# A two-layer graph network on one core: second pass in a written order, a third column block by lists, comparisons moved to ScalarE

## The chip, the cores and the metric

The kernel runs on one core of one Trainium2 chip. The metric is the device time of one execution in microseconds, the median over several executions. A profile is one further execution, recorded by the hardware profiler; its time is given beside the others.

The engines are named as the profile names them: PE is TensorE (matrix products; PEld its weight loads), DVE is VectorE, ACT is ScalarE, POOL is GpSimd, SP is SyncE. SP, ACT and POOL also issue DMA transfers, each from its own queue, in the order of the program; every engine executes its own instructions in the order in which they were issued to it.

## The reference

Two layers over a graph of 3327 nodes with 512 features each. The adjacency matrix is sparse, with weights, and skewed: the first nodes are hubs. It has ones of self-loops on its diagonal before it is weighted.

```python
def reference(x, adj, W1, b1, W2, b2, W_sa, a_sa, W_gcnb, b_gcnb, Wa, ba, Wb, bb):
    # layer 0
    h = relu(layernorm(x))
    x = x + adj @ (relu(adj @ (h @ W1) + b1) @ W2) + b2
    # layer 1
    h = relu(layernorm(x))
    t = adj @ h
    attn_a = sigmoid(concat([t, h], 1) @ Wa.T + ba)
    attn_b = sigmoid(concat([t, h], 1) @ Wb.T + bb)
    hw = h @ W_sa
    s = (hw @ a_sa[0, :512])[:, None] + (hw @ a_sa[0, 512:])[None, :]
    e = where(adj != 0, exp(-leaky_relu(s, 0.01)), 0)
    x_a = e / (e.sum(1, keepdims=True) + 1e-5) @ hw
    x_b = adj @ (h @ W_gcnb) + b_gcnb
    return x + sigmoid(attn_a * x_a + attn_b * x_b)
```

`W1` is 512 x 128, so the hidden width of layer 0 is 128.

## The kernel before

The nodes are padded to 3328, which is 26 blocks of 128. The adjacency comes transposed (`adjT`, rows are sources). Its columns, the target nodes, are cut into chunks of 512 from the back: six of 512 and one of 256 (blocks 0 and 1). Everything is float32, and PE runs a float32 matmul as two records in the profile.

**First pass** (`back` loop, lines 540 to 600). Per chunk, 26 matmuls `acc_u` (line 568) add `u = relu(layernorm(x)) @ W1` over all sources. In the first chunk the rows of `u` are made on the way (lines 322 to 336). Each adjacency tile of 128 x 512 is loaded once by SP (line 271). DVE takes from every tile the largest absolute value of each group of 32 targets (`most`, line 572). From this, `make_lists` makes for each group the list of sources that have an edge into it: flags, a running sum, a comparison of places with offsets (`at`, line 502, on DVE), small bf16 matmuls (`p_list`, line 513), then row numbers `row_h` and `row_a`. It is a generator; one step runs after each matmul of the next chunk. At a chunk's end ACT makes the Relu and `make_g` stores the block's `g` rows.

**Lists and gathers.** With the lists, POOL gathers by indirect DMA (line 166): `ae` gets the adjacency values of the listed sources (16 KB a gather), `g_row` the rows of `g` (64 KB), and in layer 1 `hr` or `rows` the rows of the finished layer (260 KB). `rooms` says how many places of 64 sources each block's list has per half: 8 for block 1, down to 3 for the last. The blocks of `OWN` load the sources of their own block directly and leave them out of the list (`extra`). If a list were longer than its places, a flag would start a dense fallback at the end (`over`, from line 1141).

**Second pass** (lines 801 to 860). It computes `adj @ g` for the seven chunks. `LISTED = 2` chunks of the back are summed by lists (`list_sums`, `acc_s`, line 784), the other five densely (`acc_g`, line 825, 26 matmuls each). Between the matmuls of a chunk, generators work on the chunk before: `make_h1` multiplies by `W2` (`px`, line 663), adds x and the bias (lines 650, 666), stores the row, makes layernorm and Relu through `ln_relu` (lines 232 to 245: statistics on DVE, root on ACT), then four weighted sums on DVE: right and left attention score (line 623) and the two gate logits of the node itself (line 630). `add_hubs` adds each finished row into the sums of block 0, which has edges from nearly everywhere (`acc_hub`, line 709, two matmuls a row, 26 rows), and `make_e_hub` makes the attention weights for it. Which generator advances is settled by remainders of the counter n, for instance `n % 3 == 2`; the scheduler may still move PE instructions against one another where nothing orders them. x is loaded when its row's turn is near (up to three rows ahead in a chunk).

**Attention stage** (from line 865). For block 25 down to block 1: `attend` gathers the rows, makes the weights on DVE and ACT; `sums` adds rows (`acc`, line 981); `copy_out` and `turn` transpose the sums (`ptt`, line 995, copied by DVE at line 1010); `weigh` multiplies by the output weights (`p_b`, line 1035, and `p_a`, line 1042); `finish` makes gates, tanh and the output. These steps are software-pipelined over blocks by hand (`queued` makes an instruction issue behind another on its engine). Remaining adjacency gathers are fetched two a block (`AE_PER`), and row gathers run 3 or 4 blocks ahead (`LEAD`).

Of the kernel before, what the change touches and what calls it, by code (L numbers as in the profile page):

```python
# [18 lines left out]
P = 128  # L19
# [6 lines left out]
EH = 8  # L26
SEG = 4
WAKE = 14
LISTED = 2
LN_EPS = 1e-5  # L30
SUM_EPS = 1e-5
SLOPE = 0.01

# [5 lines left out]
LATE = 10, 11, 16  # L39

OWN = 1, 6, 7, 8, 12, 13, 14, 15, 17, 18


def list_rooms(n_blocks):

    rooms = [0, 8, 7, 6, 5, 5] + 6 * [4]
    return (rooms + n_blocks * [3])[:n_blocks]
# [3 lines left out]
def kernel(  # L51
# [29 lines left out]
    made_order = []  # L81
    for k, c in enumerate(dense_chunks):
        for c0, w in (c, *listed_chunks[k : k + 1]):
            made_order += range(c0 // P, (c0 + w) // P)
# [3 lines left out]
    extra = [int(i in OWN) for i in range(NB)]  # L88
# [29 lines left out]
    bab_row = kept([P, 2], "bab_row")  # L118
    w_own = kept([P, 2, D], "w_own")
# [20 lines left out]
    def segments(i):  # L140

        r = rooms[i] + extra[i]
        n = -(-r // SEG)
        cuts = [-(-r * k // n) for k in range(n + 1)]
        return list(zip(cuts, cuts[1:]))
# [50 lines left out]
    def load_own(i):  # L196

        n = segments(i)[0][1]
        for h in range(2):
            rows = slice(i * P + h * HALF, i * P + (h + 1) * HALF)  # L200
            nc.scalar.dma_start(
                ae[i][h * HALF : (h + 1) * HALF, 0 : n + 1 : n, :GW],
                adjT[rows, rows].rearrange("j (q i) -> j q i", i=GW),
            )
# [41 lines left out]

    def masked_exp(e, adj):
# [11 lines left out]
    with (  # L259
        tc.tile_pool(name="l0", bufs=1) as l0,  # L260
        tc.tile_pool(name="l0w", bufs=2) as l0w,
        tc.tile_pool(name="adjp", bufs=8) as adjp,
    ):

        def load_adj(j, c, name, n=1):

            c0, w = c
            t = adjp.tile([P, CW], F32, tag="adj", name=f"{name}_{c0}_{j}")
# [26 lines left out]
        def load_weights():  # L295
# [3 lines left out]
            nc.scalar.dma_start(w_own, w_self.partition_broadcast(P))  # L299
            nc.scalar.dma_start(bab_row, b_ab.partition_broadcast(P))  # L300
# [6 lines left out]
        def load_x(i):  # L307
            xs[i] = l0w.tile([P, D], F32, tag="x", name=f"x_{i}", bufs=5)
# [47 lines left out]
        def kept0(shape, name, dtype):  # L356
            return l0.tile(shape, dtype, tag=name, name=name)
# [16 lines left out]
        def make_constants():  # L374
# [36 lines left out]
            for r in sorted(set(rooms[1:])):  # L411
                i0, n = rooms.index(r), rooms.count(r)
# [9 lines left out]
                )  # L422
            yield
# [9 lines left out]
        def make_lists(nth, most):  # L433
# [5 lines left out]
            def small(shape, name, dtype, bufs=2):  # L439
                return l0w.tile(shape, dtype, tag=name, name=f"{name}_{c0}", bufs=bufs)  # L440
# [3 lines left out]
            for b in range(w // P):  # L444
                if extra[c0 // P + b]:
                    groups = slice(b * NQ, (b + 1) * NQ)
                    own = flag[:, groups, c0 // P + b]
                    nc.vector.tensor_tensor(own, own, apart, ALU.mult)

# [18 lines left out]
            nc.vector.tensor_copy(offset[:, :n], p_off[:, :n])  # L468
# [853 lines left out]
```

## Time and profile before

| | |
|---|---|
| executions shown | 737.31, 735.01 and 1862.7 us |
| median | 737.31 us |
| profiled execution | 834.5 us; span from first to last instruction 832.8 us |
| mean granted PE clock in the profile | 0.94 |

The groups that matter, from the list of instructions by line with shapes kept apart (times in the profiled execution):

| group | count | busy us | mean ns |
|---|---|---|---|
| `acc_u`, 512 columns, line 568 (PE) | 312 | 147.6 | 614 |
| `acc_g`, 512 columns, line 825 (PE) | 208 | 104.4 | 636 |
| `acc_s`, line 784 (PE) | 192 | 11.2 | 289 |
| `acc_hub`, line 709 (PE) | 104 | 53.1 | 593 |
| `p_b` and `p_a`, lines 1035 and 1042 (PE) | 632 | 193.5 | |
| `most`, 512 columns, line 572 (DVE) | 156 | 102.7 | 676 |
| `at`, 192 columns, line 502 (DVE) | 56 | 13.7 | 300 |
| weighted sums, line 623 (DVE) | 52 | 35.6 | 684 |
| table loads (ACT) | 18 | 23.1 | 1283 |

Busy time counts overlapping instructions once, the mean does not. A matmul that has to share the array with the one before it shows a mean longer than its pace; the pace is read from a run of them in the chain. Where the engine stood still, the chain of waits says what it stood for: a name of an instruction or a transfer, "issue" where the profile shows nothing, and "another core or an unknown queue" where the release has no visible origin.

### The profile page before, as it was taken

Reading aid. Unit: us, or ns where it says so; the run is one execution under the profiler, and the core shown is the slowest. Engines: PE = TensorE matmul, PEld = TensorE weight load, DVE = VectorE, ACT = ScalarE, POOL = GpSimd, SP = SyncE. Lnnn points to the kernel's source line nnn. Section 1 sums busy time; section 2 is a strip of 40 time slices with the busy share of each in tenths; the row PEclk is TensorE's granted clock in tenths of the full one; section 3 lists DMA queues with packets and bytes.
Section 4 is the critical chain, followed back from the end, with each engine's and each line's share of the span. In section 5 each row is a group of like instructions: output and inputs, shape, how many; then the busy total and the mean of one; then the engine's idle time right before and its main releaser. Section 6 shows DMA issues by size and latency. Waiting matters only on the chain.

```text
span 832.8 us, 11907 instructions
## 1 busy us (share of the span) xinstructions
PE 735.6 (88%) x3595; PEld 404.5 (49%) x3595; DVE 506.0 (61%) x1625; ACT 194.5 (23%) x402; POOL 461.1 (55%) x490
## 2 busy tenths in 40 slices
PE   9999888989899771999899749967999999999995
PEld 7774333444543220444355236633656655665554
DVE  7778868898860611798987225523665557553552
ACT  7770000000000110354544002211212222221121
POOL 2201756766657776534456766674657666767500
PEclk9999989999999875999999969996999999999999
DMA  8788988988878844789994755664667877767510
GB/s 271 245 287 259 326 246 242 293 272 246 232 232 284 262 132 134 240 279 312 327 314 135 241 150 145 199 185 115 195 211 244 255 206 233 240 205 234 178 51 29
DMA packets 104889, 185.08 MB, mean 222 GB/s; under 512 B 18401, under 2 KB 35441, under 8 KB 104818
## 3 DMA queue, kind: packets, MB, share of 16 engines
q1 hardware_dynamic: 66544, 113.43, 41.8%
q0 software_dynamic: 23264, 57.64, 24.3%
q10 hardware_dynamic: 15010, 13.18, 4.9%
q8 instruction: 30, 0.49, 0.2%
q14 instruction: 41, 0.34, 0.1%
HBM read 162.29 MB, written 22.26 MB: 222 GB/s over the span
## 4 chain that ended last, share of the span: by engine, by line
PE 72%; DVE 7%; issue 6%; another core or an unknown queue 6%; DMA 5%; ACT 2%; POOL 1%; SPq 1%; DVEq 0%; ACTq 0%; POOLq 0%
PE acc_u L568 17%; PE acc L981 12%; PE p_b L1035 11%; PE p_a L1042 10%; PE acc_g L825 8%; PE pu L333 3%; PE ptt L995 3%; DMA a<-in_adjT_dram 2%; PE acc_hub L709 2%; PE px L663 2%; PE pt L325 1%; DMA xb<-in_x_dram 1%; PE acc_s L784 1%; DMA hr<-h_rows,row_h 1%
## 5 line engine op out<-in xcount | busy, mean ns | idle before, releaser
L166 POOL DMA_INDIRECT ae<-in_adjT_dram,row_a x194 | 202.6, 1044 | 181.8 <-DVE past L519 54.3
L568 PE MATMUL acc_u<-a,rows 128*128 128x512 f32 (+1 forms) x364 | 161.0, 583 | 0.5 <-DMA a<-in_adjT_dram 0.5
L166 POOL DMA_INDIRECT hr<-h_rows,row_h x120 | 122.7, 1022 | 62.5 <-issue 27.4
L825 PE MATMUL acc_g<-a,g 128*128 128x512 f32 (+1 forms) x260 | 117.1, 584 | 7.2 <-DMA a<-in_adjT_dram 6.8
L572 DVE TENSOR_REDUCE most<-a 128x16 f32<-128x512 f32 (+1 forms) x182 | 112.3, 638 | 11.6 <-issue 6.3
L1035 PE MATMUL p_b<-W_g_sb,tyT 128*128 128x257 f32 x416 | 99.3, 391 | 15.8 <-DVE tyT L1010 15.3
L1035 PEld LDWEIGHTS p_b<-W_g_sb,tyT 128*128 128x128 f32 x416 | 77.8, 192 | 46.5 <-DVE tyT L1010 15.6
L166 POOL DMA_INDIRECT rows<-h_rows,row_h x74 | 75.1, 1015 | 44.3 <-PE acc L981 20.9
L568 PEld LDWEIGHTS acc_u<-a,rows 128*128 128x128 f32 x364 | 67.2, 195 | 58.8 <-issue 56.0
L1042 PE MATMUL p_a<-W_sa_sb,tyT 128*128 128x512 f32 (+2 forms) x216 | 94.2, 577 | 0.2
L1010 DVE COPY tyT<-ptt 128x512 f32<-128x512 f32 x51 | 34.8, 685 | 87.0 <-PE p_a L1042 31.7
L825 PEld LDWEIGHTS acc_g<-a,g 128*128 128x128 f32 x260 | 50.0, 200 | 58.5 <-issue 44.9
L981 PE MATMUL acc<-hr,ae 64*64 64x512 f32 x480 | 68.3, 614 | 4.4 <-issue 4.0
L166 POOL DMA_INDIRECT g_row<-g_rows,row_h x48 | 49.0, 1021 | 20.9 <-issue 13.4
L1042 PEld LDWEIGHTS p_a<-W_sa_sb,tyT 128*128 128x128 f32 x216 | 40.7, 189 | 38.8 <-issue 36.9
L884 ACT ACTIVATE f<-f 128x2 f32<-128x2 f32 x26 | 5.3, 203 | 192.4 <-DVE f L883 97.2
L981 PEld LDWEIGHTS acc<-hr,ae 64*64 64x64 f32 x480 | 27.6, 136 | 33.6 <-issue 33.0
L343 ACT ACTIVATE gT<-acc_u,b_col 128x512 f32<-128x512 f32 (+1 forms) x7 | 4.6, 656 | 163.8 <-DMA a<-in_adjT_dram 90.9
L663 PE MATMUL px<-W_sb,sT 128*128 128x512 f32 x52 | 26.7, 650 | 15.4 <-ACT sT L799 12.0
L666 DVE TENSOR_TENSOR xb<-px,xb 128x512 f32<-128x512 f32 x26 | 17.3, 682 | 36.6 <-PE px L663 28.5
L981 PE MATMUL acc<-rows,ae 64*64 64x512 f32 x296 | 37.1, 593 | 2.5 <-issue 2.3
L623 DVE SCALAR_TENSOR_TENSOR junk<-rows,w_rows 128x512 bf16<-128x512 f32 x52 | 35.6, 684 | 3.2 <-ACT rows L244 1.1
(159 smaller groups left out, 945.2 us busy)
## 6 DMA issues: line engine op xcount, KB each, us to landing
a<-in_adjT_dram SPq DMA_DIRECT2D x286, 256.0 KB
h_rows<-rows SPq DMA_DIRECT2D x26, 260.0 KB
x<-in_x_dram SPq DMA_DIRECT2D x26, 256.0 KB
xb<-in_x_dram SPq DMA_DIRECT2D x26, 256.0 KB
x<-xb ACTq DMA_DIRECT2D x26, 256.0 KB
x1b<-x SPq DMA_DIRECT2D x26, 256.0 KB
out_dram<-va SPq DMA_DIRECT2D x25, 256.0 KB
ae<-in_adjT_dram,row_a POOLq DMA_INDIRECT x194
```

Of the source, the lines that this page charges most:

```text
L166: return nc.gpsimd.indirect_dma_start(out=dst, out_offset=None, in_=table, in_offset=bass.IndirectOffsetOnAxis(ap=rows, axis=0), bounds_ch ...
L333: nc.tensor.matmul(pu[:, :HID], hT[:, k, :], W1_sb[:, k, :], start=(k == 0), stop=(k == KD - 1))
L568: added = nc.tensor.matmul(acc[:, :w], u[j], a[:, :w], start=(j == 0), stop=(j == NB - 1))
L572: nc.vector.tensor_reduce(most[:, : w // GW, j], a[:, :w].rearrange("p (b i) -> p b i", i=GW), axis=AX.X, op=ALU.max, apply_absolute_value ...
L623: return nc.vector.scalar_tensor_tensor(junk, h, 1.0, w_rows[:, s, :], op0=ALU.mult, op1=ALU.mult, accum_out=into)
L663: last_row[2] = nc.tensor.matmul(px, sT[:, b * P : (b + 1) * P], W2_sb, start=True, stop=True)
L825: added = nc.tensor.matmul(acc[:, :w], g[j], a[:, n % per, :], start=(n == 0), stop=(n == NB - 1))
L981: added = nc.tensor.matmul(taken[i]["acc"][h][q * HALF : (q + 1) * HALF, :], both[half_p, q * n + k, :], taken[i][k0][k][half_p, q, :D], s ...
L995: moved = nc.tensor.transpose(pt[:, k * P : (k + 1) * P], ty[h][:, k * P : (k + 1) * P], ident)
L1010: last = nc.vector.tensor_copy(dst, src)
L1035: nc.tensor.matmul(p_b[n][:, :WH], tyT[:, k, 0, :], W_g_sb[:, k, n * WH : (n + 1) * WH], start=(k == 0), stop=(k == KD - 1),)
L1042: last = nc.tensor.matmul(p_a[:, c0:c1], tyT[:, k, 1, :], W_sa_sb[:, k, c0:c1], start=(k == 0), stop=(k == KD - 1),)
```

## The change

The change touches all stages.

- `LISTED` goes from 2 to 3: chunks of 12 blocks (14 to 25) are summed by lists, so four chunks stay dense. `made_order`, the order in which rows are finished, is written out (`MADE`: d is a dense chunk, l a listed one).
- Blocks 9, 21 and 24 (`TOP`) take the sources 0 to 63 as a whole, loaded directly, besides their own; their lists have one place less. `segments` lets five places be one segment.
- In the first pass, adjacency tiles are loaded in pairs (512 KB) into six buffers of twice the size, in place of eight single ones; the group maxima of two tiles are one instruction (not in the first chunk). The comparison `at` is a steep sigmoid on ACT.
- The second pass follows `PLAN`: d a dense matmul, s and t steps of the list sums, x a row of `make_row`, l the turning of scores, h a hub matmul, e a hub weight. Each step's PE instructions are issued behind those of the step before (`behind_pe`). After 1.4 us of planned work one gather is issued, held until the PE step of that moment is done (`gather_one`).
- The buffers that the first pass alone used are given back after the first dense chunk; eight x buffers take their place, and x is loaded six rows ahead.
- A row's layernorm takes its mean from the sum that the addition of `px` accumulates, its variance from a Square on ACT with an accumulated sum, and its reciprocal root from Ln and Exp. Left scores are made in the second pass only for blocks 0 and 22 to 25, and gate logits not at all; both are made in the attention stage from each block's own row, loaded by SP (`load_row`, `own_scores`, `turn_score`).
- At the start of the attention stage block 0's sums are turned as soon as the first half is complete, and the first blocks' sums stand between its two products (`first_sums`).

```diff
-LISTED = 2
+LISTED = 3
+MADE = "dldldld"
+SPACE, QUIET = 1.4, 8.0
+STEP = {"d": 0.93, "x": 0.93, "h": 0.93, "s": 1.1, "t": 0.6, "l": 0.5, "e": 0.0}
...
-OWN = 1, 6, 7, 8, 12, 13, 14, 15, 17, 18
+TOP = 9, 21, 24
+OWN = TOP + (1, 6, 7, 8, 12, 13, 14, 15, 17, 18)
...
-        tc.tile_pool(name="adjp", bufs=8) as adjp,
+        tc.tile_pool(name="adjp", bufs=6) as adjp,
...
-                        nc.vector.tensor_scalar(
+                        nc.scalar.activation(
                             at[:, k : k + r, h, :],
                             place_row[:, : r * HALF].rearrange("p (k m) -> p k m", m=HALF),
-                            offset[:, b : b + 1], None, op0=ALU.is_ge,
+                            AF.Sigmoid, bias=offset[:, b : b + 1], scale=STEEP,
                         )
...
+    def ln_relu_by_sum(dst, src, ln):
+        nc.vector.tensor_scalar(ln[:, 1:2], ln[:, 0:1], -1.0 / D, None, op0=ALU.mult)
+        nc.scalar.activation(dst, src, AF.Square, bias=ln[:, 1:2], accum_out=ln[:, 2:3])
+        nc.scalar.activation(ln[:, 3:4], ln[:, 2:3], AF.Ln, bias=eps, scale=1.0 / D)
+        nc.scalar.activation(ln[:, 4:5], ln[:, 3:4], AF.Exp, scale=-0.5)
+        nc.vector.tensor_tensor(ln[:, 0:1], ln[:, 1:2], ln[:, 4:5], ALU.mult)
+        return nc.scalar.activation(dst, src, AF.Relu, bias=ln[:, 0:1], scale=ln[:, 4:5])
...
+        def make_row():
+            i = next(made)
+            load_next()
+            add_b2()
+            x1 = xs.pop(i)
...
+                with behind_pe():
+                    on_pe[0] = last_row[2] = nc.tensor.matmul(
+                        px, sTs.pop(i), W2_sb, start=True, stop=True
+                    )
...
+        def gather_one():
+            with queued(g_last[0]):
+                n = g_count["taken"]
+                if n < len(g_slots) and n // NU * NU < g_count["summed"] // NU * NU + GR:
+                    made = gather_g()
+                else:
+                    made = next(columns, None)
+            if made is not None:
+                pace(made, on_pe[0])
+                g_last[0] = made
...
+        for what in plan:
+            does[what]()
+            owed[0] += STEP[what]
+            left -= STEP[what]
+            if owed[0] >= SPACE and left > QUIET:
+                owed[0] -= SPACE
+                gather_one()
...
+        def own_scores(i):
+            if i not in s_left:
+                nc.vector.scalar_tensor_tensor(
+                    junk, h_own[i][:, :D], 1.0, w_left, op0=ALU.mult, op1=ALU.mult,
+                    accum_out=node[i][:, 0:1],
+                )
+            own_logits(i, h_own[i], junk)
```

## The prediction

> **What bounds the kernel now.** First the page: busy shares of the engines, then the chain of work that ended last.
>
> ```profile
> PE 735.6 (88%) x3595; PEld 404.5 (49%) x3595; DVE 506.0 (61%) x1625; ACT 194.5 (23%) x402; POOL 461.1 (55%) x490
> PE 72%; DVE 7%; issue 6%; another core or an unknown queue 6%; DMA 5%; ACT 2%; POOL 1%; SPq 1%; DVEq 0%; ACTq 0%; POOLq 0%
> ```
>
> TensorE (PE) is busy 88% and holds 72% of the chain, so its work is the first thing to count. Next the stages, from windows cut at the stage borders: columns are PE, weight loads, DVE, ACT and POOL busy time with their instruction counts, then granted clock, DMA share and GB/s.
>
> ```profile
> 63.30:237.00 173.70, 155.23 (x732) 74.88 (x731) 146.76 (x388) 4.86 (x8) 103.64 (x101) 0.95 0.86 261
> 237.00:265.00 28.00, 26.25 (x90) 11.06 (x90) 7.18 (x22) 0.59 (x1) 19.41 (x19) 0.94 0.89 299
> 265.00:300.00 35.00, 25.78 (x109) 10.35 (x107) 17.00 (x51) 4.00 (x8) 25.03 (x25) 0.85 0.69 215
> 300.00:345.00 45.00, 24.74 (x72) 10.88 (x73) 13.25 (x42) 8.57 (x19) 26.18 (x27) 0.66 0.49 152
> 345.00:400.00 55.00, 52.78 (x227) 23.95 (x226) 47.07 (x161) 26.57 (x43) 25.67 (x23) 1.00 0.90 293
> 400.00:447.00 47.00, 43.56 (x135) 24.07 (x134) 39.45 (x132) 22.32 (x39) 25.63 (x26) 1.00 0.81 273
> 490.00:746.00 256.00, 243.65 (x1339) 145.02 (x1340) 134.33 (x481) 55.15 (x122) 167.04 (x165) 0.96 0.67 201
> ```
>
> The first row is the first pass after its opening column: PE 89%, VectorE (DVE) 84%, DMA 86%, three near-limits together, ACT nearly idle. The next five are the second pass: where it flows (345 to 447) PE is at 94% and DVE at 85%; between 265 and 345 every compute engine and the DMA fall together. The last is the attention stage: PE 95%. Then the ordered chain, for what stood there, and prices of one piece of PE work (start, length, what; matmuls of float32 are recorded as two):
>
> ```profile
> 318.65 13.65 another core or an unknown queue
> 413.81 2.58 PE acc_g L825 x6
> 473.05 16.46 another core or an unknown queue
> 585.37 3.49 PE acc L981 x30
> ```
>
> At 473 PE has finished a transpose whose copy on DVE starts only 15 us later; ACT and DVE resume together although POOL issues all the while. "Issue" and "unknown queue" are 12% of the chain, 832.8 x 0.12 = 100 us. The profiled execution took 834.5 us (span 832.8 plus 1.7), the median is 737.3: 97 us apart. I choose to read these freezes as belonging to the profiled execution, since nothing the kernel does explains them and their sum fits. Estimate of what remains: PE work at full clock, summed from row prices (first pass 205, second pass with hub sums 178, attention stage 26 blocks x 8.3 plus 107 list places x 0.87, 309), is about 690 us, so the unprofiled run holds some 45 us of idle PE. About 20 of them are the opening (8 less 6 of warming), the hand-over to attention (about 4), late gathers in the last big blocks (about 7) and the tail (7); the rest lies in the passes.
>
> Last, the gathers:
>
> ```profile
> L166 POOL DMA_INDIRECT hr<-h_rows,row_h x120 | 122.7, 1022 | 62.5 <-issue 27.4
> L166 POOL DMA_INDIRECT rows<-h_rows,row_h x74 | 75.1, 1015 | 44.3 <-PE acc L981 20.9
> ```
>
> One takes 1.02 us and the next follows 0.30 us later: 1.30 us each. From the first row gather (455) on there are 216, 281 us against some 330 of PE work: POOL is the second limit of that stage.
>
> **What the Trainium skill says.** "ScalarE: Activation LUTs", What ACT_TABLE_LOAD costs: a table switch is 1283 ns plus a drain, and an activation with a per-partition bias costs about 280 ns + 0.833 ns an element. The trace has 18 loads of 1283 ns and 806 ns for the 512-column Relu with pointer scale and bias (the page gives 280 + 427 + 93 for the second pointer, 800). The same page, Table sets, puts ln and exp in one set; no run here shows it yet. "DMA: Bandwidth & Descriptors", Issuing engines are not separate DMA queues: all queues share 16 engines; the trace agrees, 0.86 to 0.90 busy while sync, scalar and POOL queues run together. "TensorE: Matmul & The Clock Gate", What's actually happening: the clock halves after an idle window of 3.4 us; clock 0.66 in the 300 to 345 window agrees.
>
> **The change, part by part.**
>
> *Third listed chunk.* Dense sums drop one chunk: 26 matmuls x 0.86 (2.58/3) = -22.4 us. Lists add 68 small matmuls (100 to 168), 136 records x 0.045 (24 records took 1.09 us) = +6.2, and four transposes, +0.5. Three blocks (9, 21, 24) take the hubs' rows whole: one gathered place less, two whole places more, net 12 attention matmuls, 24 records x 0.116 = +2.8. Twelve fewer list-making matmuls are under 0.3. **Sum on PE: -13.** PE sets the pace there, so I count all of it. Capacity: counted from the inputs, the fullest list of 21 and 24 needs 128 places of 128, so the fallback is not entered.
>
> *Gathers.* Rows 194 to 188, adjacency 194 to 188, g rows 48 to 68: 444 for 436. By the built order 105 (before 101) come ahead of the first g gather, 113 (119) in the second pass, 226 (216) in the attention stage: POOL there 294 us instead of 281. The paced form makes each gather of the second pass wait for a PE step; queued behind it on POOL are only later gathers, and the lists' sums wait for those. Cost: nothing while 294 stays under PE's 330; without that cover, up to +13.
>
> *First pass.* 100 comparisons (56 of 192 columns at 300 ns, 24 of 256 at 296, 20 longer) go from DVE to ACT: their busy time, overlaps taken out, is about 24 us. On ACT, by the page's price, 52 x 0.44 + 20 x 0.49 + 28 longer = about 48 us, in a stretch where ACT is busy 5 of 174; nothing but the chunk-end Relu and its stores queue behind them, and the list matmuls wait for them as they now wait for DVE. The 130 maxima after the first column become two-row ones: 676 and 408 ns for 512 and 256 columns give 0.14 us fixed each, so 65 x 0.14 = 9 less. DVE falls from 147 to about 114 of 174. PE (155, some of it at lower clock) and DMA (0.86) stay: at DMA full the stage would still need 150. Worth 0 to 20; **I take -6**, a quarter of the 18.5 us of PE idle there, rounded up, because DMA is late next. Loads are 512 KB in pairs, twelve tiles deep instead of eight; the bytes are the same.
>
> *Rows of the second pass.* Per row DVE drops statistics and reciprocal (0.68 + 0.17 + 0.15 + 0.15); 21 left scores (0.76) and 13 rows' own logits (1.67) move out; it gains an accumulator read and two one-column ops (about 0.38): -30 - 16 - 22 + 10 = -58 of 124 us. ACT gains Square, Ln and Exp for one Sqrt, about 1.1 x 26 = 29 of 148 idle, and loses at least five table loads. x comes six rows ahead, in memory that the first pass's lists must have left: five x loads wait on SP for that, with the adjacency loads behind them; six 512 KB tiles, 12 matmuls or 10 us, are ahead and cover it; uncovered, +0 to +5. SP issues 131 adjacency loads for 286, and 16 more own rows in the attention stage. DVE was at 85% beside PE at 94%, so **I take -2** beyond the matmuls; from 0 to -8.
>
> *Moved into attention.* DVE gets (21 + 26) x 0.76, 36 us, on 52% of 256: hidden; if not, it delays the transposes' copies, +0 to +10. DMA: 16 x 260 KB more, 6 x 266 less, 2.6 MB on 201 GB/s against 332 seen. Left-score transposes number 26 as before. **0.**
>
> *Hand-over.* 20 hub steps (52 - 32) x 0.86 = 17 us stay behind the last row, and block 0's weights fill the wait for first rows: of the 4 idle **I take -3**; 0 to -6. Merged five-place segments save five small chains on DVE, hidden.
>
> Sum: -13 - 6 - 2 - 3 = -24. Against the profiled 834.5 that would be 810, with freezes as they fell; carried as microseconds to the median, 737.3 - 24 = **713**.
>
> **Rivals.**
>
> *POOL ends the attention stage.* For it: 1.30 us is unbroken over long stretches, and POOL's waits on PE (20.9 + 23.7) total 45, about the freezes of the stage, so an unfrozen run may leave POOL no slack. Against it: the last gather starts at 784, 48 us before the end, so PE still has work. Then the ten added gathers give back up to 13 and the hand-over gains nothing: 737 - 21 + 10 = 726, 720 to 734.
>
> *The written order stops PE.* Every step of the second pass now issues behind the one before on PE; a row not ready at its turn stops all behind it: sums, hub steps, then the paced gathers and their lists. The row's own chain is about 4 us (0.77 + 0.15 + 0.7 + 0.3 + 0.3 + 0.15 + 0.8 + 0.77). For it: two waits for x of 5 us in the chain now. Against it: DVE halves and x is earlier. At 1.6 us a row, 26 x 1.6 = 42 us: 713 + 42 = 755, 742 to 775. It decides from (24 + 15)/26 = 1.5 us a row (15 is 2%).
>
> *The freezes are real.* Then the second pass holds 35 us that a better order could remove: 690 or a little below; against it, the medians.
>
> **Chances.** Main 0.57 (own range 703 to 722); POOL 0.24; stopped PE 0.12; real freezes 0.07. Range 697 to 736 leaves out most of the last two. About 2% (15 us, 722.6) is what a measurement tells from no change: faster 0.66, the same 0.23, slower 0.11.
>
> **What would show it.** In the second pass 78 wide acc_g matmuls for 104, PE over 94% in its windows, DVE near 50%. First pass: the maxima's group half as many, comparisons under ACT, PE idle down by about 6. Attention: PE waits for gathered rows short, POOL's waits on PE still there; if PE waits for row gathers grow by 10 us, the first rival holds; if px or hub matmuls wait for ACT or DVE, the second. I am wrong if the freezes in the profile recur unprofiled, or if lists on ACT arrive late.

## The result, and the profile after

| | median us | range, executions | ratio to the kernel before |
|---|---|---|---|
| before, beside it | 736.16 | | 1 |
| after | 792.67 | 787.42 to 797.05, 4 | 1.0791, 95% interval 1.0687 to 1.0894 |

The change made the kernel slower by 56 us, outside the range that was predicted. The profiled execution took 791.3 us (span 789.6).

On some chips the kernel before takes 733 to 736 us, on others 827 to 840 us, and the 834.5 us of the profile shown with the prediction fits the latter, so times are compared only within one set of runs on one chip, each set with its own runs of the kernel before.

The base for comparing profiles is therefore a new profile of the kernel before (experiment 1, span 732.5). First the busy line and the shares of the chain of waits, of before from that run and then of after:

```profile
PE 701.0 (96%) x3595; PEld 392.1 (54%) x3595; DVE 506.6 (69%) x1625; ACT 193.9 (26%) x402; POOL 469.7 (64%) x490
PE 73%; DVE 13%; DMA 11%; ACT 1%; issue 1%; POOL 0%; SPq 0%; POOLq 0%; DVEq 0%; ACTq 0%
```

```profile
PE 711.2 (90%) x3695; PEld 386.4 (49%) x3695; DVE 465.2 (59%) x1405; ACT 311.9 (40%) x644; POOL 475.5 (60%) x516
PE 64%; ACT 14%; DMA 11%; DVE 5%; issue 3%; POOL 1%; ACTq 1%; SPq 0%; POOLq 0%; DVEq 0%
```

DVE is relieved, from 507 to 465 us. But ACT, nearly absent from the chain before, now holds 14% of it, and its busy time grew by 118 us. Then the windows from the first pass's settled part to its end, and from there to the first row sums of the attention stage (columns as in the prediction), of before and of after:

```profile
63.00:216.40 153.40, 144.66 (x719) 68.37 (x718) 141.94 (x376) 4.54 (x8) 101.96 (x99) 1.00 0.94 290
216.40:415.10 198.70, 187.51 (x695) 88.30 (x693) 140.62 (x466) 68.42 (x125) 145.41 (x133) 0.98 0.89 295
```

```profile
63.00:232.70 169.70, 153.96 (x708) 71.98 (x708) 122.98 (x221) 42.64 (x105) 101.59 (x100) 0.94 0.84 262
232.70:463.50 230.80, 182.15 (x787) 87.67 (x786) 95.16 (x326) 140.94 (x234) 135.93 (x132) 0.90 0.72 235
```

The loss has three places: the first pass is 16 us longer (169.7 for 153.4), the second pass with the hand-over 32 us longer (230.8 for 198.7), and the attention stage, 326.1 us from the first row sums to the end for 317.4, 9 us longer. No stage gained. In the attention stage most of the 9 us is work of PE itself, which is busy for 313.6 us there for 308.0. The groups on ACT name a first suspect (busy us, mean ns, idle before):

```profile
L266 ACT ACT_TABLE_LOAD x26 | 33.4, 1283 | 0.5
L267 ACT ACT_TABLE_LOAD x24 | 30.8, 1283 | 0.4
```

Lines 266 and 267 are the Ln and the Exp of a row's layernorm. Nearly every row loads a table for each of them: 50 loads, 64 us. All in all the profile has 57 loads; the kernel before has 20, of which 18 lie in its second pass. The change preloads the set that holds both functions, but it does so at the end of the last chunk, and the comparisons of that chunk's lists, which are sigmoids, come after it on ACT and displace the set (line 656 is the preload, 533 the sigmoid):

```profile
233.84 1.28 ACT L656 ACT_TABLE_LOAD   x1 [0.85 <-issue]
236.55 1.28 ACT L533 ACT_TABLE_LOAD   x1 [1.43 <-DVE size L500]
```

From then on the built program loads one set for Ln and another for Exp, and each displaces the other. The engine's timeline of one row (start, length, what) shows how it stands:

```profile
404.00 0.72 ACT L265 ACTIVATE rows<-xb,ln_b 128x512 f32<-128x512 f32 x1 [0.83 <-DVE ln_b L264]
...
405.03 1.28 ACT L266 ACT_TABLE_LOAD   x1
406.32 0.29 ACT L266 ACTIVATE ln_b<-ln_b,eps 128x1 f32<-128x1 f32 x1
406.64 1.28 ACT L267 ACT_TABLE_LOAD   x1
407.93 0.20 ACT L267 ACTIVATE ln_b<-ln_b 128x1 f32<-128x1 f32 x1
408.36 0.81 ACT L269 ACTIVATE rows<-xb,ln_b 128x512 f32<-128x512 f32 x1 [0.23 <-DVE ln_b L268]
```

From the Square (line 265) to the Relu (line 269) 4.4 us pass, of which 2.6 are loads. The alternating loads already stand in the built program, in the order of ACT's instructions, and could have been read there.

### The profile page after: what moved, and what is told of

Read it like the earlier page. It is cut to its first block, busy times and chain, and to the rows that moved or that the text cites. A ratio compares the mean times of both kernels' runs of the same rounds, so it can differ in the third digit from the quotient of the medians.

```text
span 789.6 us, 11919 instructions
## 1 busy us (share of the span) xinstructions
PE 711.2 (90%) x3695; PEld 386.4 (49%) x3695; DVE 465.2 (59%) x1405; ACT 311.9 (40%) x644; POOL 475.5 (60%) x516
## 4 chain that ended last, share of the span: by engine, by line
PE 64%; ACT 14%; DMA 11%; DVE 5%; issue 3%; POOL 1%; ACTq 1%; SPq 0%; POOLq 0%; DVEq 0%
PE acc_u L599 14%; PE acc L1112 12%; PE p_b L1166 12%; PE p_a L1174 11%; PE acc_g L903 4%; ACT L266 3%; DMA xb<-in_x_dram 3%; PE pu L358 3%; PE ptt L1126 3%; DMA ae<-in_adjT_dram 3%; ACT L267 2%; ACT rows L269 2%; DMA a<-in_adjT_dram 2%; ACT rows L265 2%; DMA W_sa_sb<-in_W_sa_dram 2%
## 5 line engine op out<-in xcount | busy, mean ns | idle before, releaser
L606 DVE TENSOR_REDUCE most<-a 128x32 f32<-128x1024 f32 (+1 forms) x104 | 104.1, 1011 | 32.5 <-DMA a<-in_adjT_dram 31.9
L179 POOL DMA_INDIRECT g_row<-g_rows,row_h x68 | 70.4, 1036 | 39.2 <-issue 14.1
L903 PE MATMUL acc_g<-a,g 128*128 128x512 f32 (+1 forms) x208 | 86.7, 559 | 1.3 <-DMA a<-in_adjT_dram 1.3
L533 ACT ACTIVATE at<-place_row,offset 128x192 bf16<-128x192 f16 (+6 forms) x100 | 39.5, 481 | 49.0 <-DMA ae<-in_adjT_dram 43.6
L903 PEld LDWEIGHTS acc_g<-a,g 128*128 128x128 f32 x208 | 39.3, 196 | 39.0 <-issue 34.4
L1112 PE MATMUL acc<-hr,ae 64*64 64x512 f32 x480 | 56.1, 592 | 0.0
L1048 ACT COPY s_left<-pl 64x64 f32<-64x64 f32 x42 | 8.7, 206 | 119.8 <-PE pl L1044 119.5
L965 DVE SCALAR_TENSOR_TENSOR a_hub<-h_own,w_own 128x512 f32<-128x512 f32 x52 | 35.5, 682 | 8.9 <-DMA h_own<-h_rows 8.8
L686 DVE TENSOR_TENSOR xb<-xb,b_row 128x512 f32<-128x512 f32 x26 | 17.9, 690 | 36.7 <-DMA xb<-in_x_dram 36.7
L753 PE MATMUL acc_hub<-rows,a_hub 128*128 128x512 f32 x52 | 30.1, 677 | 9.6 <-ACT rows L269 9.6
```

The source lines that it names most:

```text
L179: return nc.gpsimd.indirect_dma_start(out=dst, out_offset=None, in_=table, in_offset=bass.IndirectOffsetOnAxis(ap=rows, axis=0), bounds_ch ...
L533: nc.scalar.activation(at[:, k : k + r, h, :], place_row[:, : r * HALF].rearrange("p (k m) -> p k m", m=HALF), AF.Sigmoid, bias=offset[:, ...
L606: nc.vector.tensor_reduce(most[:, : w // GW, j : j + both], tiles.rearrange("p k (b i) -> p b k i", i=GW), axis=AX.X, op=ALU.max, apply_ab ...
L753: return nc.tensor.matmul(acc_hub[k], s, made_row(i)[:, :D], start=(n == 0), stop=(n == NB - 1))
L903: on_pe[0] = nc.tensor.matmul(acc[:, :w], g[j], a[:, n % per, :], start=(n == 0), stop=(n == NB - 1))
L965: nc.vector.scalar_tensor_tensor(junk, h[:, :D], 1.0, w_own[:, s, :], op0=ALU.mult, op1=ALU.mult, accum_out=node[i][:, 1 + s : 2 + s],)
```

## The experiments

The theory after the first reading: three separate causes, each hiding the next. (a) The tables hold up the rows. (b) In the first pass the comparisons stand on ACT's in-order queue behind the own-block loads, whose issue waits. (c) x reaches the rows late. The rivals: a sigmoid of 0.44 us is itself too slow; the written order leaves PE nothing to do between rows; DMA is saturated. "Chip A" is the one where before takes 733.1 us, "chips B" are four where it takes 827 to 840, "chip C" is one of 734.3.

**Before, once more (chip A).** The kernel before is unchanged; the run asks whether the stretches without any engine in the first profile belong to the kernel.

> The kernel before, unchanged, for a second profile. If the freezes of the first profile (about 100 us in which all compute engines stood still) belonged to that one execution, the span here is near 735 us and the chain of waits holds little unknown time. If they belong to the profiler or to the kernel, the span is again above 800 us.

734.25 us, span 732.5, clock 0.99. Apart from the last 5.5 us, the longest stretch in which PE, DVE and ACT all stood still was 1.1 us. The kernel has no long stretches of its own. On chips B they recur in every profile, the longest, 5 to 11 us, near the start of the attention stage. The chain shows one as this piece:

```profile
443.35 15.07 another core or an unknown queue
```

The line is from the chain of the run with the bias behind (below); in its 15 us all three engines stand for 10.7. What the stretches come from is not visible in the trace and stays open. Nor are they the whole difference between the chips: those over 1.5 us add up to 39 us in the profile shown with the prediction, which took 100 us longer than this one, and PE was busy there for 735.6 us instead of 701.0.

**One table load (chip A).** The preload is issued behind the last comparison.

```diff
-        with queued(chunk_end):
-            nc.scalar.preload_act_table_set("natural_log_exp_and_others")
...
+                        last_at[0] = nc.scalar.activation(at[...], ...)
...
                     for _ in lists:
                         pass
+                    with queued(last_at[0]):
+                        nc.scalar.preload_act_table_set("natural_log_exp_and_others")
```

> The changed kernel with one line moved: the table set that holds both Ln and Exp is loaded after the last sigmoid comparison instead of before it, so the 50 table loads of the rows (64 us of ScalarE time) should become one. Theory 1 (the table loads bind the second pass): its length falls from 236 us towards 185, the time to 740 to 750 us. Theory 2 (the written order stops PE for other reasons: late x, late lists): the loads were beside other waits, and the time stays above 775 us. Theory 3 (comparisons stuck on ScalarE's queue): the first pass keeps its 15 us of PE waits for comparisons, whatever the second pass does.

762.55 us, ratio 1.0418 (1.034 to 1.0495), after 1.0791: by the ratios 27 us of the loss are gone, and so are the 50 loads; four loads are left in the whole kernel. From the first pass's end to the first row sums it takes 197.9 us for 230.8. One line was moved, so (a) is shown, with its size. The waits of this run (engine, line, what it waited for: us, times, longest) name the next cause:

```profile
ACT at L535 <- DMA ae<-in_adjT_dram: 44.0, 4, 20.7
PE p_list L546 <- ACT at L535: 16.4, 7, 9.2
```

and the timeline shows what ACT was doing while PE waited for a comparison:

```profile
96.89 13.97 ACTq L216 DMA_DIRECT2D ae<-in_adjT_dram  x10
110.97 2.18 ACT L535 ACTIVATE at<-place_row,offset 128x192 bf16<-128x192 f16 x6 [20.74 <-DMA ae<-in_adjT_dram]
111.47 0.23 PE L546 MATMUL p_list<-step,at 128*64 128x27 bf16 x1 [9.15 <-ACT at L535]
```

Ten loads of 16 KB each occupy ACT's queue for 14 us; the comparisons behind them start when the last is issued, and PE's list matmuls stop for 9 us. The wait costs more than itself: it lies from 102.3 to 111.5, and from 106.9 to 120.6 the granted clock was 0.50, so PE did its next 9 us of work at half the clock.

**Comparisons on DVE (chip A).** The comparison is again what the kernel before has; since no sigmoid intervenes, the tables stay too.

```diff
-                        nc.scalar.activation(
+                        nc.vector.tensor_scalar(
                             at[:, k : k + r, h, :], place_row[...],
-                            AF.Sigmoid, bias=offset[:, b : b + 1], scale=STEEP,
+                            offset[:, b : b + 1], None, op0=ALU.is_ge,
```

> The changed kernel with the comparisons back on VectorE. No sigmoid is then left, so the combined table set stays loaded too. Theory 1 alone: the same time as the run with the table loaded once, within 5 us. Theory 3: 10 to 20 us less than that run, since PE no longer waits for comparisons that stand behind DMA issues on ScalarE's queue; about 725 to 735 us. If VectorE is the limit of the first pass, as the forecast had it, the time is instead 5 us or more above that run.

741.6 us, ratio 1.0114 (1.0073 to 1.0155): another 21 us less. The first pass ends at 218.0 for 233.2 with one table load and 216.4 in the kernel before. What remains is 8.5 us over the kernel before, although PE has a chunk less to do. By place it is the attention stage, 326.2 us for 317.4; the second pass with the hand-over, which was to gain, takes 198.0 us for 198.7. DVE's wait for x there points to why it does not gain:

```profile
DVE xb L684 <- DMA xb<-in_x_dram: 61.8, 22, 7.5
```

**Own-block loads later, more x buffers, an earlier transpose (chips B).** Three edits, each alone: the own-block loads issued behind the next chunk's comparisons (on the kernel with one table load); `X_BUFS = 12` (on the kernel with comparisons on DVE); `turn_score` before `turn` (on the same).

```diff
-                for i in OWN:
-                    if n and (c0 <= i * P < c0 + w or ...):
-                        load_own(i)
+                if j == NB - 4:
+                    with queued(last_at[0]):
+                        for i in due:
+                            load_own(i)
...
-X_BUFS = 8
+X_BUFS = 12
...
+                added = turn_score(i - 1) or added
+            with queued(added):
                 ...
-            with queued(added):
-                added = turn_score(i - 1) or added
```

> Beside the run with the table loaded once (762.6 us): the loads of the blocks' own adjacency (32 small transfers on ScalarE's queue) are issued after the chunk's comparisons instead of before them; comparisons stay on ScalarE. If the comparisons stood behind these issues, each of which waits for an earlier transfer, PE's 16 us of waits for comparisons fall under 5 us and the time is 743 to 750 us. If ScalarE is simply a slower place for comparisons (0.44 us each instead of 0.30), the time stays at 758 us or more.

> Beside the run with comparisons on VectorE (741.6 us): twelve x buffers instead of eight, so x is loaded ten rows ahead. If x is late because a load must wait until the row before it in its buffer has been stored (46 us of waits on SP's queue, 62 us of VectorE waits for x), those waits fall by more than half and the time is 730 to 736 us. If x is late because the DMA engines are full with adjacency then, nothing is gained: 739 to 744 us.

> Beside the run with comparisons on VectorE (741.6 us): in the attention stage the turning of a block's left scores stands before the transposes of the sums instead of between the small sums of weights and the row sums. A four-place block takes 12.03 us there and 11.67 us in the kernel before. If the single transpose costs by its place (0.25 us and the lost overlap of the small sums), 22 blocks gain 0.2 to 0.3 us each: 735 to 738 us. If it costs 0.36 us wherever it stands, the time stays within 2 us; if the scores are not ready so early, it is above 745 us.

824.67, 818.09 and 812.63 us beside 828.08 for the kernel before: ratios 0.9917, 0.9840 and 0.9800, intervals within 0.9 points of each. On this chip all three come out below the kernel before, so these ratios can't be set against those of chip A, and no base of theirs ran beside them. Bases and two combinations ran on another chip B:

> The kernel with one load of the combined table set again, beside the one with the loads moved behind the comparisons, on one chip: the same as before (1.042 on a chip of 733 us); it is the base from which the own-block loads are counted.

> The own-block loads behind the next chunk's comparisons, on the same chip as its base with one table load. Theory: 13 to 16 us less than that base, first pass 155 instead of 169 us from 63, PE wait for p_list a few us. Rival (the comparisons themselves are late on ACT, by their price and their order): under 4 us less.

> Four edits on the changed kernel at once: one load of the combined table set behind the last comparison; the own-block loads issued behind the next chunk's comparisons; twelve x buffers for eight; the left-score transpose ahead of the block's four row transposes. Comparisons stay on ACT. Theory (the loss is the sum of four separate waits): first pass as the kernel before's or a little shorter (comparisons free of the loads ahead of them), PE wait for p_list under 4 us, DVE wait for x (was 61.8 us) under 35, row transposes still 0.36 us late per block or less; against the kernel before 0.97 to 0.99 on a chip where that takes 733 us. Rival (ACT itself is too slow for comparisons and rows): first pass over 165 us from 63, ratio above 1.01.

> Comparisons on DVE as in the kernel before, twelve x buffers, the left-score transpose early. Theory: 1.0114 of the run with only the comparisons moved, less about 5 us for x and 3 to 6 us for the transposes: ratio 0.995 to 1.003 on a chip of 733 us. If DVE's relief in the first pass is worth what the prediction gave it (6 us), this is 6 us slower than the same with comparisons on ACT and unblocked; if it is worth nothing, they are equal within 4 us.

| chip B, before 828.89 us | median us | ratio (interval) |
|---|---|---|
| one table load | 831.49 | 1.0036 (0.9977 to 1.0096) |
| and own-block loads later | 822.61 | 0.9921 (0.9869 to 0.9973) |
| and twelve x buffers, early transpose | 822.01 | 0.9916 (0.9860 to 0.9973) |
| comparisons on DVE, twelve x buffers, early transpose | 820.32 | 0.9894 (0.9837 to 0.9951) |

Moving the own-block loads is worth 9 us there, against 13 to 16 forecast and under 4 for the rival that a sigmoid is too slow; the intervals just fail to overlap. So the order of ACT's queue is the cause of (b), though here it is worth less than thought. Comparisons on ACT, unblocked, and on DVE differ by 2 us, less than can be told apart. Twelve x buffers did not shorten the wait: DVE waited 53.2 us for x in that run, and 38.5 and 39.1 us in two profiles with eight buffers on another chip B (below). That miss led to a closer look at (c).

**Why more buffers didn't help.** This is part of the built order on DVE, of the changed kernel, with only the lines of x kept (the number is the place among DVE's instructions); line 686 adds b2 to a loaded x, line 705 adds px:

```
501 L686 xb_20 <- xb_20, b2_row
506 L705 xb_4  <- px_4, xb_4
511 L686 xb_21 <- xb_21, b2_row
515 L705 xb_5  <- px_5, xb_5
519 L686 xb_8  <- xb_8, b2_row
523 L705 xb_6  <- px_6, xb_6
526 L686 xb_9  <- xb_9, b2_row
530 L705 xb_7  <- px_7, xb_7
535 L686 xb_10 <- xb_10, b2_row
540 L705 xb_18 <- px_18, xb_18
```

The code asks for the addition of b2 two rows ahead. The scheduler, which nothing tied, put it six rows ahead (the rows go 18, 19, 20, 21, 8, 9, 10), as far ahead as the load. So the "six rows ahead" of the load are used up: DVE stands at the bias of row k+6 and can't add px to row k. With eight buffers the load of row k+6 itself waits until row k-2 is stored. The chain of the run with comparisons on DVE walks round this ring (lines between left out):

```profile
274.83 6.38 DMA xb<-in_x_dram
281.24 0.74 DVE xb L684
281.98 0.62 DVE xb L703 x2
...
293.79 7.62 DMA x<-xb
...
301.47 2.87 DMA xb<-in_x_dram
304.43 0.69 DVE xb L684
```

Load, bias, px added, store of x1 (`x<-xb`), next load. In this chain a load takes 3 to 6 us, a store 6 to 8, and two rows must carry both: from first to last finished row (the start of its Relu) 135.3 us, 5.41 us for each of 25 steps. With twelve buffers the code loads ten rows ahead (`X_BUFS - 3`, and one), and by the same order the bias would follow the load there too, so that the ring is as tight as before; that wait of 53.2 us fits this.

**The bias behind (chips B).** The addition of b2 is issued behind the px addition of two rows earlier, with comparisons on DVE and the early transpose; the same on ACT with all four repairs (table load, own-block loads, transpose, bias); and their base and the early transpose alone on the same chip.

```diff
             load_next()
-            add_b2()
             x1 = xs.pop(i)
...
-                nc.vector.scalar_tensor_tensor(
+                added = nc.vector.scalar_tensor_tensor(
                     x1, px, 1.0, x1, op0=ALU.mult, op1=ALU.add, accum_out=ln[:, 0:1]
                 )
...
+            with queued(added):
+                add_b2()
```

> Comparisons on DVE, left-score transpose early, eight x buffers, and each addition of b2 to x issued behind the addition of px two rows before. In the changed kernel's built order on DVE the addition of b2 for a row stands ahead of the px addition of a row six before, so DVE waits for the load just issued, which waits for the store of the row eight before: two rows have to carry a load of 4 us and a store of 7. Theory (this ring sets the row period of 5.4 us): DVE wait for x under 15 us for 62, rows done in 105 to 115 us for 135, second pass 15 to 25 us shorter; against the kernel with the transpose early alone -12 to -20 us. Rival (x is late because the adjacency tiles ahead of it saturate the DMA, whose share is 0.99 to 1.05 up to 300 us): DVE's wait only moves to the px addition; under 4 us.

> As the kernel with the bias behind, with the comparisons on ACT, one table load behind the last of them, and the own-block loads behind the next chunk's comparisons. Theory: as above, and equal to it within 4 us if DVE's relief in the first pass is worth nothing; 6 us or more below it if the prediction's step for the first pass was right and only blocked.

> Only the comparisons on DVE, on the same chip as the others: the base. DVE wait for x near 62 us, row period 5.4 us.

> The base with the left-score transpose ahead of the block's row transposes. Theory (a single small transpose between two groups costs 0.36 us in each of 22 blocks): 6 to 9 us under the base, all in the attention stage. Rival (the records only show it there): within 2 us.

| chip B, before 836.38 us | median us | ratio (interval) |
|---|---|---|
| comparisons on DVE | 826.88 | 0.9899 (0.9830 to 0.9968) |
| early transpose | 828.26 | 0.9887 (0.9852 to 0.9921) |
| early transpose, bias behind | 823.45 | 0.9860 (0.9785 to 0.9934) |
| the same, comparisons on ACT, unblocked | 827.84 | 0.9887 (0.9822 to 0.9952) |

In time all four are the same within their intervals: the 12 to 20 us forecast for the bias did not show. In the trace DVE's wait for x fell, but another took its place. First the line of the early transpose alone, then two of the same with the bias behind:

```profile
DVE xb L684 <- DMA xb<-in_x_dram: 39.1, 17, 7.4
```

```profile
DVE xb L684 <- DMA xb<-in_x_dram: 13.1, 2, 7.6
DVE xb L702 <- PE px L698: 23.2, 4, 12.2
```

DVE's wait for px, 4.1 us with the early transpose alone, is now 23.2. So the rows came no closer together, 5.70 us each for 5.62 (5.98 in the base), and the last came 185 us after the first pass for 188. That is what the rival "DVE's wait only moves to the px addition" says, and on chips B it holds. There are stretches of 4.0 and 4.2 us among the rows in which no engine worked; whether they hide a gain can't be told there. Two more runs of this kernel fell on chips B as well:

> The kernel with comparisons on DVE, the left-score transpose early and the bias behind, once more. On a chip where the kernel before takes 733 us and the profile shows no stretches without any engine, theory: 1.0114 of the kernel with the comparisons moved, less 6 to 9 us in the attention stage and 5 to 12 us in the second pass: ratio 0.982 to 0.996. On a chip where the kernel before takes 828 us, where those stretches swallow part of any gain: 0.98 to 0.99, as measured.

> The same kernel as in the run before, for a chip without the stretches in which no engine works. There, theory: ratio 0.982 to 0.996; from the end of the first pass to the last finished row 160 to 168 us where the kernel with the comparisons moved took 174 and the kernel before 177; from the first row sums to the end 317 to 320 us for 326. Rival (PE, not the ring, set the pace of the rows): 172 us or more to the last row.

812.19 us beside 826.93 (0.9816, 0.9706 to 0.9925) and 823.06 beside 840.15 (0.9882, 0.9756 to 1.0009); a row every 5.89 and 5.73 us, the last 187 and 188 us after the first pass.

**The changed kernel and the repaired one (chip C).** The kernel after itself, and the one with all four repairs and the comparisons on ACT, which had run on a chip B (827.84 us above).

> The changed kernel itself beside the repaired one. On a chip where the kernel before takes 733 us: 1.07 to 1.09. On one where it takes 830 us, with stretches in which no engine works: the kernel with one table load came to 1.004 there for 1.042, so 1.03 to 1.05, if those stretches swallow some 26 us of any loss of this kind.

> All repairs with the comparisons on ACT: one table load, own-block loads behind the comparisons, bias behind, left-score transpose early. On a chip of 733 us, theory: ratio 0.98 to 0.995; first pass 150 to 156 us from 63, last row 160 to 168 us after it. If DVE's relief in the first pass is worth the 6 us of the prediction, the first pass is 148 us or less. On a chip of 830 us: 0.98 to 0.99.

788.98 us (1.0786, 1.0708 to 1.0864) and 732.8 us (0.9972, 0.9947 to 0.9997) beside 734.3. The four repairs take away 56 us, the whole loss of 55 and little more; 0.98 to 0.995 was expected. The comparisons are still on ACT, so a sigmoid as such is not what the change lost by. The profile of the repaired kernel is of one execution of 740 us, 7 above the median. PE waits 3.6 us for comparisons in it (15.0 in the changed kernel), and DVE's wait for x in the second pass is small:

```profile
DVE xb L693 <- DMA xb<-in_x_dram: 9.6, 2, 5.2
```

The window from its first pass's end to the first row sums beside the same of the run with comparisons on DVE, which comes second:

```profile
226.30:408.70 182.40, 169.87 (x786) 83.35 (x784) 92.88 (x325) 71.98 (x181) 135.90 (x130) 0.98 0.88 295
```

```profile
218.00:416.00 198.00, 174.15 (x786) 85.39 (x784) 95.80 (x331) 68.26 (x177) 137.59 (x133) 0.95 0.84 276
```

DMA's share of 0.88 here, where the rows come faster, for 0.84 speaks against the rival that DMA was saturated. The stages of the three profiles (a row counts as finished when its Relu starts, the hub sums when the last of their matmuls starts):

| us | before | comparisons on DVE | repaired |
|---|---|---|---|
| first pass to last finished row | 177.5 | 174.1 | 154.3 |
| first pass to end of the hub sums | 195.4 | 188.8 | 168.9 |
| first pass to first row sums | 198.7 | 198.0 | 182.4 |
| first row sums to the end | 317.4 | 326.2 | 329.5 |

The rows now come every 4.56 us, and the last is finished 20 us earlier than in the run with comparisons on DVE. The kernel with one table load, which has its comparisons on ACT as well, needed 175.4 us to the last row, so their place alone is not what shortened it. Besides the bias, the own-block loads of the last chunk and the transpose differ. The bias alone did not run on such a chip, and the same repaired kernel took 5.72 us a row on a chip B. So that the ring of loads and stores cost the 20 us is the likeliest reading, not shown: it rests on one profile, and the experiment with the bias alone speaks against it on chips B.

Half of the 20 us is not seen in the time: by the ratios, 1.0114 and 0.9972, the repaired kernel is 10 us faster. In the profiles 4 us go to the hand-over (13.5 us from hub sums to row sums for 9.2) and 3 to the attention stage; the first pass of this one profile is 8 us longer, with a granted clock of 0.57 from 205 to 228 us.

**What takes it back.** In the attention stage of the repaired kernel the chain leaves PE, which it doesn't in the kernel before:

```profile
648.27 3.59 DMA hr<-h_rows,row_h
...
654.14 0.77 POOL rows L179
...
655.44 4.12 DMA rows<-h_rows,row_h
...
660.67 5.28 DMA rows<-h_rows,row_h
```

From 647 to 688 PE runs at the pace at which POOL issues gathers. From the first row gather to the last POOL issues 226 of them, from 394.7 to 702.0, without a pause over 0.6 us; in the kernel before 216, from 399.3 to 687.9. Ten more gathers and a slightly longer pace (1.36 for 1.34 us) make the stream 19 us longer, and it starts only 5 us earlier, because 14 us pass between the last finished row and the first row gather, in which POOL issues adjacency gathers. By this reading an earlier start of PE's sums would not end the stage earlier; no run with fewer gathers tests it.

POOL explains only the last 3 us, though. In the run with comparisons on DVE the chain stays on PE from 600 to 712, and its stage is 8.8 us longer than in the kernel before all the same: PE is busy for 313.7 us there for 308.0.

The single transposes are part of that work. The chain over one block of four places, in the kernel before, with comparisons on DVE, and in the repaired kernel:

```profile
562.97 0.05 PE acc L981
...
563.03 3.49 PE acc L981 x30
...
574.49 0.15 PE p_b L1018 x2
```

```profile
566.73 0.25 PE pl L1042
566.98 3.60 PE acc L1110 x32
570.57 3.67 PE p_b L1164 x16
574.24 3.43 PE p_a L1172 x8
577.67 0.87 PE ptt L1124 x8
578.55 0.21 PE p_b L1147 x4
578.76 0.25 PE pl L1042
```

```profile
557.49 0.11 PE pl L1056
...
569.27 0.11 PE pl L1056
```

A block takes 11.67 us (574.64 - 562.97) before, 12.03 (578.76 - 566.73) with the left-score transpose between two small groups, 11.78 (569.27 - 557.49) with it ahead of the row transposes. Over 21 blocks that would be 7.6 us and then 2.3, an estimate from these blocks. In the times the early transpose can't be seen: on a chip B it took 828.26 us beside 826.88 without.

## Why the prediction was wrong, point by point

Two steps failed and account for most of the 56 us: what ACT's queue does with the tables in the second pass (27 us), and what stands ahead of the comparisons on it in the first (21 us). A third, that less work on PE is less time, is why the gain forecast did not come.

- **Third listed chunk, -13 on PE.** The work was sized well. In the run with comparisons on DVE the wide dense sums fell from 99.2 to 73.1 us (-26.1, forecast -22.4), and list sums with their transposes rose from 9.5 to 16.4 (+6.9, forecast +6.7). What failed is "PE sets the pace there, so I count all of it". The attention stage starts when the last row has been finished, stored and gathered, and that one was finished after 174.1 us for 177.5: PE's idle time from the first pass to the first row sums grew from 11 to 24 us.
- **"Loses at least five table loads".** This is the step that cost most. The sign was wrong: the loads rose from 20 to 57, and those of the rows were worth 27 us. With the preload in its place the loads fall to four, so the step would have held. The preload was read from the diff as if it held until the rows; which function stands between was not followed on ACT's queue.
- **"Nothing but the chunk-end Relu and its stores queue behind them".** The prediction asked what stands behind the comparisons, not what stands ahead: up to ten own-block loads, 14 us at a time. "If lists on ACT arrive late", which the prediction named as a sign of being wrong, is what happened: PE waited 15.0 us for comparisons, 1.7 in the kernel before. Removing the comparisons from that queue gave 21 us. Their price was right: 441 and 494 ns for 192 and 256 columns, 0.44 and 0.49 us forecast. The -6 for DVE's relief did not show once they were unblocked: on chips B the kernels with comparisons on ACT came out 2 and 4 us slower than those on DVE, which is less than can be told apart. DVE's busy time in the first pass fell by 19 us, from 142 to 123 (33 forecast), PE's rose from 145 to 154 under a lower clock, and DMA was already at 0.94.
- **"x comes six rows ahead".** True of the load, and made worthless by the addition of b2, which the built order puts six rows ahead as well. The +0 to +5 kept for x was for SP's queue; the wait was on DVE's, 61.8 us in the run with comparisons on DVE. What it cost in time is not shown: 20 us up to the last row between two profiles on chips A and C, nothing on chips B.
- **"Left-score transposes number 26 as before. 0."** The number is right, the neighbours are not: 0.36 us in a block, where one was shown. With the +2.8 that was counted for attention places this is about the 9 us by which the stage is longer in the changed kernel and in both runs with edits on chip A.
- **Hand-over, -3.** It became slower: 9.2 us from hub sums to row sums for 3.3, and 13.5 in the repaired kernel. Finished rows don't help until their gathers come, and those stand behind adjacency gathers on POOL.
- **The freezes.** Rightly not of the kernel; but not of the one profiled execution either, as the prediction chose to read them. Every profile on chips B has them, and every execution there is some 95 us longer. "Their sum fits" did not hold: the stretches over 1.5 us add up to 39 us in that profile, not 97. On those chips the same loss is smaller: one table load came to 1.0418 on chip A and 1.0036 on B.
- **The rivals.** "The written order stops PE" was the right mechanism on the right side: a row not ready at its turn stops all behind it. It was priced at 42 us over the forecast and given 0.12; the evidence against it, "DVE halves and x is earlier", looked at how long the engines work and not at the order in which they stand. "POOL ends the attention stage", 726, shows in the chain of the repaired kernel, with exactly the 226 for 216 gathers that were counted, but for some 3 us; that 732.8 lies in its range is in part luck, as PE's own work made the stage longer too.

## What to carry to other kernels

Where a change puts work on an engine with an in-order queue, read the built order there in both directions: what now stands behind the new work, and what already stands ahead of it, table loads and DMA issues included. A load made early is only as early as the first operation that reads it, if that one stands in order on an engine: look where it was scheduled. When a wait disappears, look whether it came back under another name before counting it as gained. Before counting less work as less time, find the chain by which the next stage starts, and ask what bounds that stage if it starts earlier.

## What the hardware showed that was not expected

- A combined table set holds Ln and Exp, as the Trainium skill says ("ScalarE: Activation LUTs", Table sets), but only while it is the loaded one: with a sigmoid after the preload 50 loads of 1283 ns appeared, with the preload behind the last sigmoid they were gone. The drain that the prediction named beside each load is not to be seen in the row shown: from the end of the Ln (406.61) to the start of the Exp (407.93) 1.32 us pass, 1.28 of them the load.
- Ten DMA issues of 16 KB on ACT's queue held it for 14 us while earlier transfers were under way, and the 9 us for which PE then stood were followed by 9 us of work at half the clock.
- Shorter idle times than the 3.4 us that the prediction names lowered the clock: in the new profile of before PE has three idle stretches over 2 us, of 2.5, 2.9 and 2.7 us (from 292.6, 342.4 and 412.4), and at or just after the end of each (from 295.2, 346.4 and 414.6) the granted clock was 0.50 for 3.4 us.
- The same kernel takes 733 us on one chip and 827 to 840 on others, with stretches of up to 15 us in which ACT waits for nothing that the trace shows while POOL goes on issuing for most of them. What a change gains on one kind of chip can't be read off its times on the other: the four repairs bring 1.0786 down to 0.9972 on chip C, and the repaired kernel is at 0.9887 on a chip B.
